# A ring of eight rows of mixing weights, and two projections in groups of 64 columns

## The chip, the core and the metric

The kernel runs on one core of one Trainium2 chip. The metric is the device time of one execution in microseconds. A profile shows each engine of the core: TensorE (PE, with its weight loads as PEld), VectorE (DVE), ScalarE (ACT), GpSimd (POOL) and SyncE (SP, which only starts transfers here). All arithmetic is float32; the query-key products alone read operands that VectorE has rounded and split into a high and a low part (`fp32r`).

## The reference

The input `x` has 4 images of 64 channels and 96 x 96 pixels. Two layers follow each other, each added to its input.

```python
# layer 0: attention without softmax, then a gate per channel
h = groupnorm(x)                       # 32 groups of 2 channels
q, k, v = wq @ h, wk @ h, wv @ h       # 8, 8 and 64 channels, N = 9216 pixels
att = sigmoid(q.T @ k)                 # [N, N] per image
out = v @ att.T + h
x = x + out * sigmoid(mlp(mean(out)) + mlp(max(out)))
# layer 1: a spectral convolution
u = rfft2(groupnorm(x))                # along w, then along h
top = einsum('bchw,cohw->bohw', u[:, :, :16, :16], R_pos)
bot = einsum('bchw,cohw->bohw', u[:, :, -16:, :16], R_neg)
x = x + irfft2(zeros with top and bot put in)
```

Layer 0 is nearly all of the work: for every image a 9216 x 9216 matrix is made, put through a sigmoid and multiplied by the values. In layer 1 only 32 x 16 frequencies of each channel are kept, so its transforms are small matrix products. At each kept frequency a 64 x 64 complex matrix of its own mixes the channels. These mixing weights (`spec`) come to 32 rows of 512 KB, one for each frequency along h.

## The kernel before, in words

The images go through in two pairs; two images of 64 channels fill the 128 partitions. A pair has 18 blocks of 512 queries, so there are 36 blocks, and each block goes over 72 chunks of 128 keys for both images: 144 tiles of 128 keys by 512 queries.

The loop (`for t in range(T)`) handles a burst of 6 or 7 tiles at a time. `energies` (L432) multiplies keys by queries into PSUM banks, ScalarE's `sigmoids` (L443) writes the attention tiles to SBUF in two instructions, and `attend` (L461) multiplies values by earlier tiles. Values of image b are 64 columns wide, so the matmuls of the two images go in turn to columns 0 to 63 and 64 to 127 of the array and accumulate in one bank. The lists `DENSE`, `HALF` and `SPARSE` give the burst sizes of a block: a burst of 7 uses all banks, and a burst of 6 leaves one bank over (`bank_a`). Everything else that TensorE does goes through that bank: `mid[t]` and `end[t]` hold the side steps of burst t, and `put` hands a chain of steps to the next free bursts of 6. `later` tells the framework's scheduler not to issue a step before the last marked vector instruction. Within that, the scheduler decides the order of instructions on each engine: it works with its own estimate of when operands are there, and lets other ready work of the same engine go first.

The side steps that matter here:

- In the two `DENSE` blocks, `keys` (L392) and `values_of` (L401) make keys and values of a pair, a block of 512 pixels at a time. `values_of` has four matmuls in which 128 pixels are the stationary operand (128 columns) and `wv` the moving one. `queries` (L412), `keys` and `attend` each put their output in two halves of 64 partitions.
- Layer 1 of the first pair (`Hidden`) runs in the free bursts while the second pair's attention goes on. Its order is: transposes (L266), transform along w (L276), group statistics, transform along h (L303), mixing (`mix`, L203), transform back along h (`back_h`, L322) and back along w (`back_w`, L343), and the sum with the input.
- `mix(q, half)` takes four rows of weights, 4q to 4q + 3, each in a group of 32 columns of the array, and has eight matmuls (two column frequencies by four rows). VectorE moves the result to the buffer `vms` (L579, the lambda given as `move`); after the second half, four stores (L219) send it to the DRAM tile `vd`. There are eight q, so sixteen steps.
- `weights` (L314) loads rows on the sync queue. Four buffers are held, so the rows of q + 1 are asked for after the second half of q.
- The first pair's `x` isn't needed any more by then. `workspace` puts into its place the transformed input `ut`, four rows of weights, one `vms` buffer, and later `z`, the input of the transform back along w. Another buffer, tag `ah`, 16 KB per partition, holds the input of the transform along h and afterwards `vt`, the mixed frequencies.
- `back_w(i)` has one matmul of 128 columns with 384 moving columns for every four image rows; 24 of them. VectorE (L345) adds the layer's input, and the sync queue stores it.

The second pair's layer 1 follows after the loop and has nothing to hide behind (from L640 on).

Of the kernel before, what the change touches and what calls it, by code (L numbers as in the profile page):

```python
# [33 lines left out]
F32 = mybir.dt.float32  # L34
# [6 lines left out]
P = 128  # L41
B, C, H, W = 4, 64, 96, 96
# [4 lines left out]
KW = 16  # L47
KH = 32
# [11 lines left out]
U = KH * KW * 4  # L60
UPAD = 4 * SIDE
# [20 lines left out]
def tile_kernel(ctx: ExitStack, tc: tile.TileContext, x, cst, late, spec, out):  # L82
    nc = tc.nc
# [10 lines left out]
    xs = []  # L94
# [11 lines left out]
    def named(name, rows=P):  # L106
        return cs[:rows, PLACE[name]]
# [128 lines left out]
    class Hidden(Layer1):  # L236
# [7 lines left out]
            self.ad = dram.tile([H, 2 * KW, P], F32, tag=f"ad{p}", name=f"ad_{p}")  # L244
            self.zd = dram.tile([H, 2 * KW, 2, C], F32, tag=f"zd{p}", name=f"zd_{p}")

        def place_of_vt(self):
            return self.work.tile([P, KW * C], F32, tag="ah", name=f"vt_{self.p}")

        def result(self, s):  # L250
            p, cols = self.p, bass.ts(s, STRIP)
# [82 lines left out]
        def back_w(self, i, x1d):  # L334

            s = i // 2
            cols = bass.ts(s, STRIP)
            if i % 2 == 0:
                self.old = self.work.tile([P, STRIP], F32, tag="old", bufs=2,
                                          name=f"x1_{self.p}_{s}")  # L340
                nc.sync.dma_start(self.old, x1d[:, cols])
            py = self.bank(f"py_{self.p}_{i}")
            nc.tensor.matmul(py[:, :4 * W], self.z[:, i, :], named("gw"), start=True, stop=True)  # L343
            o = self.old[:, bass.ts(i % 2, 4 * W)]
            nc.vector.tensor_tensor(o, py[:, :4 * W], o, ALU.add)  # L345
            if i % 2:
                nc.sync.dma_start(outf[bass.ts(self.p, P), cols], self.old)


    with tc.tile_pool(name="work", bufs=1) as work, \  # L350
# [9 lines left out]
        at = attp.tile([P, 14, NB], F32, tag="at", name="at")  # L360
# [3 lines left out]
        def bank_a(name):  # L364
            return banks[:, spare[0], :]
# [17 lines left out]
        def later(step):  # L383
            with tc.issue_after(mark[0].ins):
                step()
# [11 lines left out]

        def values_of(p, s):
            pp = bank_a(f"pv_{p}_{s}")
            for i in range(4):  # L400
                nc.tensor.matmul(pp[:, bass.ts(i, P)], xs[p][:, bass.ts(4 * s + i, P)],  # L401
                                 named("wv"), start=True, stop=True)
            nc.vector.tensor_tensor(  # L403
                vT[:, 4 * s:4 * s + 4, :], pp.rearrange("p (i m) -> p i m", m=P),
                named("bv").unsqueeze(1).to_broadcast([P, 4, P]), ALU.add)

        def queries(p, n):
            pq = bank_a(f"pq_{p}_{n}")
            half = NB // 2
            for e in range(2):  # L410
                rows = bass.ts(e, P // 2)
                nc.tensor.matmul(pq[rows, :half], named("wq")[:, rows],  # L412
                                 xs[p][:, n * NB + e * half:n * NB + (e + 1) * half],
                                 start=True, stop=True)
            qu, qh = halves(pq[:, :half], named("bq"), f"q_{p}_{n}")
            q = qp.tile([P, NB], F32R, tag="q", name=f"q_{p}_{n}")
            for e in range(2):
                rows, cols = bass.ts(e, P // 2), bass.ts(e, half)
                low_or_high(q[rows, cols], qu[rows, :], qh[rows, :], low_sb[rows, 0:1])
                for b in range(2):  # L420
                    to, of = 64 * (1 - e) + 32 * b, 64 * e + 32 * b
                    nc.vector.tensor_copy(q[to:to + 32, cols], q[of:of + 32, cols])  # L422
            return q
# [59 lines left out]
        def after(p):  # L483

            f = small.tile([P, 2], F32, tag="f", name=f"f_{p}")
            hid = small.tile([2 * R, 2], F32, tag="hid", name=f"hid_{p}")
            gate = small.tile([P, 1], F32, tag="gate", name=f"gate_{p}")

            def means():
                tot = small.tile([P, 1], F32, tag="tot", name=f"tot_{p}")  # L490
                nc.vector.tensor_reduce(tot, sums[p], AX.X, ALU.add)
                nc.vector.tensor_scalar(f[:, 0:1], tot, 1.0 / N, None, ALU.mult)
                nc.vector.tensor_reduce(f[:, 1:2], maxs[p], AX.X, ALU.max)

            def hidden():
                ph = bank_a(f"ph_{p}")
                nc.tensor.matmul(ph[:2 * R, 0:2], named("w1"), f, start=True, stop=True)
                nc.vector.tensor_scalar(hid, ph[:2 * R, 0:2], 0.0, None, ALU.max)

            def gates():  # L500
                pg = bank_a(f"pg_{p}")
                nc.tensor.matmul(pg[:, 0:2], named("w2", 2 * R), hid, start=True, stop=True)
                gsum = small.tile([P, 1], F32, tag="gsum", name=f"gsum_{p}")
                nc.vector.tensor_reduce(gsum, pg[:, 0:2], AX.X, ALU.add)
                nc.scalar.activation(gate, gsum, AF.Sigmoid)

            return gate, [means, hidden, gates], f
# [6 lines left out]
        keys(0, 0)  # L514
        q = queries(0, 0)
        values_of(0, 0)
        later(norm0[2])
        keys(0, 1)
        values_of(0, 1)

        pattern = [DENSE] + [SPARSE] * (NBLK - 2) + [DENSE] + [HALF] * 12
# [10 lines left out]
        end = [[] for _ in range(T)]  # L532
# [3 lines left out]
        def put(t, steps, every=1):  # L536

            for step in steps:
                t = next(f for f in free if f >= t)
                free.remove(t)  # L540
                mid[t] += [lambda step=step: later(step)]
                t += every
            return t

        ask = {}
        for n in range(1, NPAIR * NBLK):
            t = begins[n] - 4
            if pattern[n - 1] is DENSE:
                end[t] += [lambda n=n: ask.update({n: queries(n // NBLK, n % NBLK)})]
            else:  # L550
                t = [f for f in free if f < begins[n] - 1][-1]
                free.remove(t)
                mid[t] += [lambda n=n: ask.update({n: queries(n // NBLK, n % NBLK)})]
        for s in range(2, NBLK):
            end[s - 2] += [lambda s=s: keys(0, s)]
            mid[s - 1] += [lambda s=s: values_of(0, s)]
            if s + 1 < NBLK:
                end[s - 2] += [lambda s=s: later(norm0[s + 1])]
# [8 lines left out]
        for s in range(NBLK):  # L567
            tiles = TILES * (NBLK - 1) + 8 * (s + 1)
            t = next(t for t in range(T) if done[t] >= tiles)
# [9 lines left out]
        l1 = Hidden(0, gate, bank_a, lambda dst, src: nc.vector.tensor_copy(dst, src), work)  # L579
        x1d = dram.tile([P, N], F32, tag="x1", name="x1d")  # L580
        for s in range(NSTRIP):
# [3 lines left out]
        t = put(first + 9, [step for m in range(H // 16) for step in [  # L585
            lambda r=r: l1.transposes(r) for r in range(4 * m, 4 * m + 4)] + [
                lambda m=m: l1.along_w(m)]])
        t = put(t, l1.stats_steps(), 2)

        def workspace():  # L590
            ws = xpool.tile([P, N], F32, tag="x0", name="ws")
            l1.ut = ws[:, :U + UPAD]
            at = 2080
            l1.wts = [ws[:, at + 1024 * i:at + 1024 * (i + 1)] for i in range(4)] * (KH // 4)
            l1.vms = [ws[:, at + 4096:at + 5120]] * (KH // 4)
            l1.z = ws[:, at:at + 3072].rearrange("q (h m) -> q h m", m=P)
            l1.weights(range(4))

        end[t] += [workspace]
        t = put(t + 2, [lambda i=i: l1.along_h(i) for i in range(4)], 2)  # L600
        end[t] += [lambda: later(l1.constant_mode)]

        def mixing(q, half):
            l1.mix(q, half)
            if half and q + 1 < KH // 4:
                l1.weights(range(4 * q + 4, 4 * q + 8))

        t = put(t + 1, [lambda q=q, half=half: mixing(q, half)
                        for q in range(KH // 4) for half in range(2)])
        t = put(t + 5, [lambda i=i: l1.back_h(i // 4, i // 2 % 2, i % 2) for i in range(8)])  # L610
        t = put(t + 5, [lambda i=i: l1.back_w(i, x1d) for i in range(H // 4)])
# [13 lines left out]
        for s in range(NSTRIP):  # L625
            tiles = TILES * (NPAIR * NBLK - 1) + 2 * (STRIP // P) * (s + 1)
            t = next(t for t in range(T) if done[t] >= tiles)
# [5 lines left out]
        for t in range(T):  # L633
            n = block[t]
            spare[0] = n % 2 * 7
            if t + 1 < T:
                if starts[t + 1] == 0:
                    q = ask[n + 1]
# [12 lines left out]
        gate, steps, f = after(1)  # L651
# [4 lines left out]
    with tc.tile_pool(name="tail", bufs=1, reuse_waits="tile") as tail, \  # L656
# [6 lines left out]
        def place_of(tag, name):  # L663

            return tail.tile([P, KW * C], F32, tag=tag, name=name)
# [17 lines left out]
        def occupy(n, behind, pool):  # L683
# [3 lines left out]
            with tc.issue_after(behind.ins):  # L687
                for _ in range(n):
# [3 lines left out]
        l1 = Layer1(1, gate, lambda name: small_bank.tile([P, NB], F32, tag="m", name=name),  # L692
                    evacuate, (nc.sync, nc.gpsimd, nc.scalar))
# [12 lines left out]
        for s in range(NSTRIP):  # L706
# [7 lines left out]
            n, i = divmod(s, NSTRIP // NSQ)  # L714
# [6 lines left out]
            if i < NSTRIP // NSQ - 1:  # L721
# [7 lines left out]
                                 stop=(n == NSQ - 1 and part == 1))  # L729
# [13 lines left out]
        for i in range(9):  # L743
            h = NSLOT + 9 + i
# [14 lines left out]
        t = place_of("s", "t")  # L759
# [29 lines left out]
        for i in range(4):  # L789
            for e in range(2):  # L790
                for b in range(2):
                    rows = bass.ts(b, 2 * KH)
# [3 lines left out]
                        start=True, stop=True)  # L796
# [10 lines left out]
        for g in range(SQ // HG):  # L807
            py = py_bank.tile([P, NSQ, NB], F32, tag="y", name=f"py_{g}")
            for i in range(HG):
                for j in range(NSQ):  # L810
                    rows = bass.ts(j, SQ)
# [93 lines left out]
```

## Time and profile before

The median is 3162.33 us of 3 runs (3162.15 to 3162.39). The profiled execution spans 3160.8 us.

| what | us | share of the span |
|---|---|---|
| TensorE matmul | 3116.3 | 99% |
| TensorE weight loads | 1157.4 | 37% |
| ScalarE | 2424.2 | 77% |
| VectorE | 397.7 | 13% |
| GpSimd | 24.5 | 1% |
| values times attention, L461 | 2415.9 | 76% |
| energies, L432 | 577.6 | 18% |
| value projections, L401 | 43.8 | 1.4% |
| mixing of the first pair, L203 | 30.0 | 0.9% |
| back along w, L343 | 21.9 | 0.7% |

A row of the profile names line, engine, operation and tiles. One float32 matmul leaves two matmul records, one of the energies leaves one. In the timeline, records of the same line are merged into one row while no other comes between: the columns are the start, the time from the first start to the last end, and the number of records. As matmuls overlap, the length of such a row reaches into the next; what a group costs is the distance from its start to the start of the next group. The first pair's mixing runs from 1988 to 2191 us, its transform back along w from 2331 to 2562 us, and the two dense blocks are the first (from 29 us) and the nineteenth one (key and value projections of the second pair up to 1528 us).

### The profile page before, as it was taken

The numbers are of one execution on the slowest core, as the hardware profiler recorded it, in microseconds if no ns is written. First come the engines' busy times: TensorE is split into PE (matmuls) and PEld (weight loads), VectorE is DVE, ScalarE is ACT, GpSimd is POOL, SyncE is SP. The second block draws the span as 40 slices with busy tenths as digits, with TensorE's granted clock in tenths as the row PEclk, the third lists the DMA queues.
The fourth block names the chain that finished last, engine by engine and source line by source line (L and its number), as shares of the span: only waits on it lengthen the run. The fifth ranks groups of instructions, "written<-read, shape, count | busy, mean of one in ns | idle before, by whom it ended". The sixth has DMA issues, their size and how long they took to land.

```text
span 3160.8 us, 42345 instructions
## 1 busy us (share of the span) xinstructions
PE 3116.3 (99%) x18850; PEld 1157.4 (37%) x18850; DVE 397.7 (13%) x838; ACT 2424.2 (77%) x1585; POOL 24.5 (1%) x49
## 2 busy tenths in 40 slices
PE   6999999999999999999999999999999999999998
PEld 3433333333333333334333334333333333333336
DVE  5300000000000000003231111000101100000015
ACT  3788888888888888886777777756777778888871
POOL 0000000000000000000000000000000010000001
PEclk9999999999999999999999999999999999999998
DMA  3000000000000000000120010122211030000026
GB/s 141 1 1 1 1 1 1 1 1 1 1 1 1 1 1 1 1 1 1 40 94 8 7 41 1 61 94 67 31 30 41 31 128 1 1 1 1 6 64 222
DMA packets 39158, 88.82 MB, mean 28 GB/s; under 512 B 10336, under 2 KB 17248, under 8 KB 38880
## 3 DMA queue, kind: packets, MB, share of 16 engines
q1 hardware_dynamic: 31856, 61.88, 6.3%
q0 software_dynamic: 5344, 19.27, 1.6%
q10 hardware_dynamic: 1776, 4.97, 0.4%
q8 instruction: 147, 2.41, 0.3%
q14 instruction: 35, 0.29, 0.0%
HBM read 62.77 MB, written 23.33 MB: 27 GB/s over the span
## 4 chain that ended last, share of the span: by engine, by line
PE 97%; DVE 1%; DMA 1%; issue 0%; ACT 0%; SPq 0%; POOL 0%; ACTq 0%; DVEq 0%
PE banks L461 74%; PE banks L432 16%; PE banks L401 1%; PE banks L203 1%; PE banks L412 1%; PE banks L343 1%; PE banks L392 1%; DMA x<-in_x_dram 0%; PE py L812 0%; PE pv L203 0%; PE banks L266 0%; DVE x L162 0%; DMA old<-in_x_dram 0%; DVE xt L711 0%; PE banks L322 0%; PE banks L303 0%
## 5 line engine op out<-in xcount | busy, mean ns | idle before, releaser
L443 ACT ACTIVATE at<-banks 128x1536 f32<-128x1536 f32 (+1 forms) x1548 | 2404.0, 1597 | 656.3 <-PE banks L432 564.3
L461 PE MATMUL banks<-at,vT 128*64 128x512 f32 (+1 forms) x11728 | 2415.9, 550 | 0.0
L461 PEld LDWEIGHTS banks<-at,vT 128*64 128x64 f32 x11728 | 777.1, 136 | 1361.3 <-issue 1303.6
L432 PE MATMUL banks<-q,kT 32*128 32x512 f32 x5184 | 577.6, 454 | 2.3 <-ACT at L443 1.2
L432 PEld LDWEIGHTS banks<-q,kT 32*128 32x128 f32 x5184 | 235.1, 183 | 481.2 <-issue 304.1
L466 DVE SCALAR_TENSOR_TENSOR x<-banks,x 128x512 f32<-128x512 f32 x36 | 24.9, 692 | 898.1 <-PE banks L461 898.1
L372 DVE TENSOR_SCALAR full_q<-banks,cs 128x256 f32<-128x256 f32 x36 | 17.4, 484 | 854.0 <-PE banks L412 854.0
L401 PE MATMUL banks<-cs,x 128*128 128x128 f32 x288 | 43.8, 297 | 1.5 <-DVE full_q L372 0.6
L401 PEld LDWEIGHTS banks<-cs,x 128*128 128x128 f32 x288 | 36.6, 199 | 16.2 <-DVE full_k L372 14.6
L422 DVE CAST q<-q 32x256 fp32r<-32x256 f32 x144 | 40.9, 284 | 3.9
L345 DVE TENSOR_TENSOR x<-banks,x 128x384 f32<-128x384 f32 x24 | 13.4, 558 | 200.7 <-PE banks L343 160.6
L579 DVE COPY xT<-banks 96x512 f32<-96x512 f32 x24 | 16.5, 686 | 167.4 <-PE banks L266 167.4
L380 DVE SCALAR_TENSOR_TENSOR q<-high_q,cs,full_q 64x256 fp32r<-64x256 f32 x72 | 34.6, 480 | 2.4
L579 DVE COPY ws<-banks 128x512 f32<-128x512 f32 x16 | 11.1, 692 | 181.4 <-PE banks L203 171.9
L203 PE MATMUL banks<-ws 128*32 128x256 f32 x256 | 30.0, 387 | 0.0
L372 DVE TENSOR_SCALAR full_k<-banks,cs 128x256 f32<-128x256 f32 x36 | 17.4, 484 | 98.4 <-PE banks L392 98.4
L403 DVE TENSOR_TENSOR vT<-banks,cs 128x512 f32<-128x512 f32 x36 | 24.9, 692 | 9.4 <-PE banks L401 9.2
L392 PE MATMUL banks<-x,cs 128*64 128x256 f32 x144 | 23.9, 396 | 1.6 <-DVE x L149 1.5
L468 DVE TENSOR_REDUCE maxs<-x 128x1 f32<-128x512 f32 x36 | 24.7, 686 | 1.2
L412 PE MATMUL banks<-x,cs 128*64 128x256 f32 x144 | 23.9, 410 | 0.6 <-DVE full_k L372 0.6
L474 DVE BATCH_NORM_STATS2 stats<-x 128x6 f32<-128x512 f32 x36 | 22.2, 680 | 8.1 <-DMA x<-in_x_dram 8.1
L719 PE MATMUL pa<-xt,lc 128*128 128x256 f32 x72 | 18.8, 422 | 3.6 <-DVE xt L711 2.6
(115 smaller groups left out, 441.9 us busy)
## 6 DMA issues: line engine op xcount, KB each, us to landing
ws<-in_spec_dram SPq DMA_DIRECT2D x32, 512.0 KB
x<-in_x_dram SPq DMA_DIRECT2D x15, 512.0 KB
out_dram<-x SPq DMA_DIRECT2D x18, 384.0 KB
w<-in_spec_dram POOLq DMA_DIRECT2D x10, 512.0 KB, 6.5
old<-in_x_dram SPq DMA_DIRECT2D x12, 384.0 KB
x1d<-x SPq DMA_DIRECT2D x12, 384.0 KB
x<-x1d SPq DMA_DIRECT2D x12, 384.0 KB
w_early<-in_spec_dram POOLq DMA_DIRECT2D x9, 512.0 KB, 8.0
```

The costliest lines, as they stand in the source:

```text
L203: self.last = nc.tensor.matmul(pv[bass.ts(g, 32), :].rearrange("q (n k o) -> q n k o", n=SIDE, o=C)[:, :, k, :], self.ut[:, at:at + 32], s ...
L343: nc.tensor.matmul(py[:, :4 * W], self.z[:, i, :], named("gw"), start=True, stop=True)
L372: nc.vector.tensor_scalar(u, src, bias, None, ALU.add)
L380: mark[0] = nc.vector.scalar_tensor_tensor(dst, h.bitcast(F32), is_low, u, ALU.mult, ALU.add)
L392: nc.tensor.matmul(pp[cols, :NB // 2], named("wk")[:, cols], src[:, e, :, :], start=True, stop=True)
L401: nc.tensor.matmul(pp[:, bass.ts(i, P)], xs[p][:, bass.ts(4 * s + i, P)], named("wv"), start=True, stop=True)
L412: nc.tensor.matmul(pq[rows, :half], named("wq")[:, rows], xs[p][:, n * NB + e * half:n * NB + (e + 1) * half], start=True, stop=True)
L422: nc.vector.tensor_copy(q[to:to + 32, cols], q[of:of + 32, cols])
L432: nc.tensor.matmul(banks[:, bank_of(t) + i - starts[t], :], kT[r:r + 32, i // 4, :], q[r:r + 32, :], start=True, stop=True)
L443: nc.scalar.activation(at[:, of + lo:of + hi, :], banks[:, bank + lo:bank + hi, :], AF.Sigmoid)
L461: nc.tensor.matmul(acc[half, cols], vT[:, j, half], at[:, place(2 * pair + b), cols], start=(j == 0), stop=(j == NCH - 1))
L579: l1 = Hidden(0, gate, bank_a, lambda dst, src: nc.vector.tensor_copy(dst, src), work)
```

## The change

There are three edits, of two kinds.

The ring: the workspace now holds five rows of weights. When the transform along h has read its input, the buffer `ah` is taken again as a room for three more rows and for `vt`. This makes eight buffers, and the rows of q + 2 are asked for after the second half of q. So a row's load has a whole q more of time before it is used.

The halves: a value projection's 128 pixels, and the 128 rows (two images of 64 channels) of the transform back along w, are taken as two stationary operands of 64 columns, which go to the two halves of the array like `attend`'s. The number of products is the same; there are twice as many matmuls and weight loads, each half as wide.

```diff
-        def place_of_vt(self):
-            return self.work.tile([P, KW * C], F32, tag="ah", name=f"vt_{self.p}")
+        def more_room(self):
+            room = self.work.tile([P, 2 * KW * P], F32, tag="ah", name=f"room_{self.p}")
+            rooms = [room[:, bass.ts(i, KW * C)] for i in range(4)]
+            self.wts = (self.wts + rooms[:3]) * (KH // 8)
+            self.place_of_vt = lambda: rooms[3]
...
-            nc.tensor.matmul(py[:, :4 * W], self.z[:, i, :], named("gw"), start=True, stop=True)
+            for b in range(2):
+                nc.tensor.matmul(py[bass.ts(b, C), :4 * W], self.z[:, i, bass.ts(b, C)],
+                                 named("gw"), start=True, stop=True)
...
             for i in range(4):
-                nc.tensor.matmul(pp[:, bass.ts(i, P)], xs[p][:, bass.ts(4 * s + i, P)],
-                                 named("wv"), start=True, stop=True)
+                for e in range(2):
+                    nc.tensor.matmul(pp[bass.ts(e, P // 2), bass.ts(i, P)],
+                                     xs[p][:, bass.ts(2 * (4 * s + i) + e, P // 2)],
+                                     named("wv"), start=True, stop=True)
...
-            at = 2080
-            l1.wts = [ws[:, at + 1024 * i:at + 1024 * (i + 1)] for i in range(4)] * (KH // 4)
-            l1.vms = [ws[:, at + 4096:at + 5120]] * (KH // 4)
-            l1.z = ws[:, at:at + 3072].rearrange("q (h m) -> q h m", m=P)
-            l1.weights(range(4))
+            rows = [ws[:, U + UPAD + KW * C * i:U + UPAD + KW * C * (i + 1)] for i in range(6)]
+            l1.wts = rows[:5]
+            l1.vms = [rows[5]] * (KH // 4)
+            l1.z = ws[:, U + UPAD:U + UPAD + 3072].rearrange("q (h m) -> q h m", m=P)
+            l1.weights(range(5))
+
+        def more_room():
+            l1.more_room()
+            l1.weights(range(5, 8))
...
-        end[t] += [lambda: later(l1.constant_mode)]
+        end[t] += [more_room, lambda: later(l1.constant_mode)]
...
-            if half and q + 1 < KH // 4:
-                l1.weights(range(4 * q + 4, 4 * q + 8))
+            if half and q + 2 < KH // 4:
+                l1.weights(range(4 * q + 8, 4 * q + 12))
```

## The prediction

> **What bounds the kernel now.** I read the page's first part and the chain of the work that ended last, then PE's idle by releaser, then PE's timeline in the three stages that the change touches.
>
> ```profile
> PE 3116.3 (99%) x18850; PEld 1157.4 (37%) x18850; DVE 397.7 (13%) x838; ACT 2424.2 (77%) x1585; POOL 24.5 (1%) x49
> ...
> PE 97%; DVE 1%; DMA 1%; issue 0%; ACT 0%; SPq 0%; POOL 0%; ACTq 0%; DVEq 0%
> ```
>
> TensorE (PE) is 97% of the chain. All its waits together are 44.5 us (3160.8 - 3116.3), nearly all in the first 27 us and after 3072 us; inside the loop the only ones of note are 1.16 us at 1624 and 1.19 us at 2062. So a microsecond of PE's stream saved in the loop is a microsecond of the result, and what matters is the time from one group's start to the next, not the busy sums.
>
> The dense blocks (columns: start us, length us, engine, line). One burst with a key and a value projection:
>
> ```profile
> 1452.16 0.73 PE L432 MATMUL banks<-q,kT 32*128 32x512 f32 x6
> 1452.82 1.16 PE L401 MATMUL banks<-cs,x 128*128 128x128 f32 x8
> 1453.91 2.80 PE L461 MATMUL banks<-at,vT 128*64 128x512 f32 x12
> 1456.54 0.60 PE L392 MATMUL banks<-x,cs 128*64 128x256 f32 x4
> ```
>
> Each fp32 matmul leaves two records. L401's four full-width matmuls hold PE 1.09 us (1453.91 - 1452.82). L461's six value matmuls, in two groups of 64 columns in turn, take 2.63 us: 0.43 each.
>
> The mixing of the first pair. First the two steps of the first q, then a stretch of a later one:
>
> ```profile
> 1987.49 0.73 PE L432 MATMUL banks<-q,kT 32*128 32x512 f32 x6
> 1988.15 1.07 PE L203 MATMUL banks<-ws 128*32 128x256 f32 x16
> 1989.15 2.79 PE L461 MATMUL banks<-at,vT 128*64 128x512 f32 x12
> ...
> 1996.36 1.07 PE L203 MATMUL banks<-ws 128*32 128x256 f32 x16
> ```
>
> ```profile
> 2062.55 1.07 PE L203 MATMUL banks<-ws 128*32 128x256 f32 x16
> ...
> 2073.60 0.62 PE L203 MATMUL banks<-ws 128*32 128x256 f32 x2
> 2074.15 1.07 PE L461 MATMUL banks<-at,vT 128*64 128x512 f32 x2
> 2075.15 0.73 PE L432 MATMUL banks<-q,kT 32*128 32x512 f32 x6
> 2075.81 1.07 PE L461 MATMUL banks<-at,vT 128*64 128x512 f32 x2
> 2076.81 0.62 PE L203 MATMUL banks<-ws 128*32 128x256 f32 x2
> ...
> 2083.67 1.07 PE L203 MATMUL banks<-ws 128*32 128x256 f32 x16
> ```
>
> In one piece the eight L203 matmuls take 1.00 us. Scattered, a lone one takes 0.55 (2074.15 - 2073.60), and it tears a pair of value matmuls apart, so that a lone L461 takes 1.00 instead of 0.43. No wait stands here: the cost is in the order, which has the shape of weights arriving one row at a time.
>
> The transform back along w, 24 such:
>
> ```profile
> 2331.22 0.91 PE L343 MATMUL banks<-cs,ws 128*128 128x384 f32 x2
> 2332.06 2.80 PE L461 MATMUL banks<-at,vT 128*64 128x512 f32 x12
> ```
>
> That is 0.84 us for one 384-wide matmul.
>
> **What the Trainium skill says.** "TensorEngine Tiling (Array Packing)", Key Properties: different tiles run weight loads and matmuls in parallel, and changing the tiling mode drains the engine. The trace agrees: 64-column matmuls in turn come every 0.43 us where a lone one takes 1.00, and a last L461 matmul ahead of L432 takes 0.53 instead of 0.43, 0.10 for the drain. "TensorE: Matmul & The Clock Gate", Part 3, What overlaps: matmuls stay strictly in order. So an L203 that sits between two halves of an L461 pair really parts them, as seen.
>
> **Part 1, the ring.** Eight rows instead of four: five in the workspace and three in the room that held the input of the transform along h; rows for q+2 are asked for after q. The sizes and the work are the same. What moves is PE's order: in the changed program's instruction order all sixteen mixing groups stand as eight in a row, where before seven of the sixteen (the first half of every q but the first) were split into 1, 1, 1 and 5. The cost of a split: from the second half of one q to that of the next is 21.12 us (2083.67 - 2062.55), with 26 energy matmuls. One unsplit step, with 13 of them, is 8.21 us (1996.36 - 1988.15), so two are 16.42. Saved per q 4.70 us, times 7: 32.9, say 33.
>
> Will the weights be there? Four rows, 2.1 MB, land in about 10 us at the rate of this stage:
>
> ```profile
> 2040.00:2050.00 10.00, 10.00 (x68) 3.28 (x66) 2.08 (x4) 7.33 (x6) 0.00 (x0) 1.00 0.63 211
> ```
>
> (the last column is GB/s). Before, they were wanted 8.2 us after their request, which explains the split. Now they are wanted a whole q later, 24.6 us. Rows 5 to 7 go out when the transform along h ends (about 1974 before the shift) and are wanted at the second q, 30 us on, for 1.5 MB or some 8 us. One row of each batch (q+3's first) stands ahead of the intermediate's stores on the sync queue and waits for the second half of q+1, as those stores do through the vector copy; it adds about 2.5 us to their landing, against 8.2 us until the buffer is needed. So I cost the loads at nothing, hidden behind bursts. If all of them were late, the bound is the whole 33. ScalarE has room: two 1.45 us sigmoids per burst of 3.39 us (six energies and six values).
>
> **Part 2, value projections, 36.** Four 128-column matmuls become eight of 64 columns, in turn. L401 costs 1.09, and L461's first matmul after it shows 0.48 instead of 0.43: 0.05 to enter the 64-column mode. After: a 64-column matmul 512 wide costs 0.429 in turn, a 256-wide one 0.215 (L412, L392), a 64-wide one 0.058 (L303, where two weight loads sit behind so little streaming). For 128 wide that interpolates to 0.109. So 0.05 + 8 x 0.109 = 0.92, and nothing on the following L461, since its mode is already set; this is how L461 behaves after L412. Saved 1.09 + 0.05 - 0.92 = 0.22, or 0.17 if the entry is paid twice; 36 x 0.22 = 7.8 (6.1). The first two lie in a stage that VectorE's chain also holds, which could hide half a microsecond.
>
> **Part 3, back along w, 24.** Two of 64 columns: 0.05 + 2 x 0.322 = 0.69 against 0.84, and 0.05 on the next L461: 0.20 each, 24 x 0.20 = 4.8 (3.6 with the entry paid twice).
>
> Nothing else moves: the vector, scalar and queue work is the same in number, and the tail after 3072 us isn't touched. Sum: 33 + 7.8 + 4.8 = 45.6; 3162.3 - 45.6 = 3116.7, so 3117.
>
> **Rivals.**
> - The ring pays nothing: PE waits for weights where it was split before. For it: weights are requested in bursts on one queue. Against: 24.6 us of lead on 10 us. 3162.3 - 12.6 = 3150.
> - The halves pay nothing: twice as many weight loads bind at 128 columns of streaming. For it: a load's record is 136 ns (L412), longer than the 109 ns that a group then has for each of its passes. Against: L303 has loads of 138 ns, half the streaming, and still 58 ns a pass. 3162.3 - 33 = 3129.
> - The slower side: the halves run one after the other, each at the full-width price. Value projections add 4 x 0.223 = 0.89 x 36 = 32, back along w 24 x 0.64 = 15.4; 3162.3 - 33 + 47.4 = 3177. For it: lone 64-column matmuls do cost this. Against: L461, L392 and L412 all alternate and overlap.
>
> **How the numbers follow.** My forecast 0.86, ring alone failing 0.05, halves failing 0.06, slower 0.03. Within the forecast the parts can move by some 3 us downward in gain (entries paid twice, start hidden), or up by 5 if splits cost more where the sparse blocks begin. The range of 3110 to 3130 takes in the halves failing and leaves out the other two, 0.08, and a little of the edges. Faster 0.96, within 0.2% (6.3 us) 0.01, slower 0.03.
>
> **What would show it.** L203 as sixteen groups of 16 records with 8.2 us between the steps of a q and no wait for a transfer; value groups of 16 records in about 0.92 us; the back transform's 4 records in about 0.69; PE busy near 3071. I am wrong if PE shows waits for weights at L203, if an L401 successor's group stays near 1.09, or if the vector copy holds PE's bank once bursts are closer.

## The result, and the profile after

The changed kernel takes 3117.19 us (median of 4 runs, 3114.36 to 3118.38), against 3162.34 us before (3162.15 to 3162.39): a ratio of 0.9856, with a 95% interval of 0.9839 to 0.9873. The forecast was 3117.

The page after, its first part and the chain. Line numbers have moved: L401 is now L409, L432 is L441, L461 is L470, L343 is L348; L203 has kept its number.

```profile
PE 3072.2 (99%) x19186; PEld 1147.4 (37%) x19186; DVE 397.0 (13%) x838; ACT 2424.6 (78%) x1585; POOL 24.5 (1%) x49
...
PE 97%; DVE 1%; DMA 1%; issue 0%; POOL 0%; SPq 0%; ACT 0%; POOLq 0%; DVEq 0%
```

PE has 336 records more and 44.1 us less to do, and bounds the kernel as before. A dense burst and the start of the next one, after:

```profile
1448.13 1.09 PE L409 MATMUL banks<-cs,x 128*64 128x128 f32 x16
1449.05 2.75 PE L470 MATMUL banks<-at,vT 128*64 128x512 f32 x12
1451.63 0.60 PE L398 MATMUL banks<-x,cs 128*64 128x256 f32 x4
1452.16 0.73 PE L441 MATMUL banks<-q,kT 32*128 32x512 f32 x6
1452.82 1.09 PE L409 MATMUL banks<-cs,x 128*64 128x128 f32 x16
```

From start to start a group of value projections costs 0.92 us (was 1.09), and the six value matmuls behind it 2.58 (were 2.63): the step into the 64-column mode is paid once. The whole burst takes 4.69 us (1452.82 - 1448.13), 0.22 less than before.

The mixing, after: second half of one q, then the next q (the first row of a step whose rows lie in two buffers shows one record; the next rows hold the others).

```profile
2044.66 1.07 PE L203 MATMUL banks<-ws 128*32 128x256 f32 x16
2045.66 2.80 PE L470 MATMUL banks<-at,vT 128*64 128x256 f32 x16
...
2052.21 0.73 PE L441 MATMUL banks<-q,kT 32*128 32x512 f32 x6
2052.87 0.40 PE L203 MATMUL banks<-ws 128*32 128x256 f32 x1
...
2053.87 2.80 PE L470 MATMUL banks<-at,vT 128*64 128x512 f32 x12
...
2061.08 0.40 PE L203 MATMUL banks<-ws 128*32 128x256 f32 x1
```

One step takes 1.00 us (2053.87 - 2052.87), and second half to second half is 16.42 us, where it was 21.12. The back transform:

```profile
2290.49 0.87 PE L348 MATMUL banks<-cs,ws 128*64 128x384 f32 x4
2291.19 2.74 PE L470 MATMUL banks<-at,vT 128*64 128x512 f32 x12
```

0.70 us instead of 0.84. PE's waits, longest first, hold no wait for a row of weights at L203:

```profile
PE banks L132 <- DVE mv_l L128: 19.7, 1, 19.7
PE pz L806 <- DMA vt<-vd: 3.1, 1, 3.1
PE pa L732 <- DVE xt L724: 2.6, 2, 2.4
```

Where the time came from, by the start of each block's first energy matmul in the two traces (blocks counted from 0; the second dense block is block 17, so the eighteenth and not the nineteenth, and its last two value projections run on into block 18):

| stretch | what changed in it | us saved |
|---|---|---|
| start to block 19 | 36 value projections | 7.48 |
| block 19 to 23 | nothing; PE waits longer for VectorE | -0.44 |
| block 23 to 27 | mixing | 33.67 |
| block 27 to 30 | 24 back transforms | 4.66 |
| block 30 to the last energy matmul | nothing | -0.13 |
| behind it, the second pair's layer 1 | nothing | -1.07 |

That makes 44.2, the difference of the spans (3160.8 - 3116.6). The loss before block 23 is one wait, for VectorE's copy of the first pair's transposes (`xT`), first before the change, then after it:

```profile
1624.57 0.50 PE L432 MATMUL banks<-q,kT 32*128 32x512 f32 x1 [1.16 <-DVE xT L579]
1617.52 0.49 PE L441 MATMUL banks<-q,kT 32*128 32x512 f32 x1 [1.59 <-DVE xT L588]
```

The last row of the table was not followed up; it is less than the 4.0 us by which the runs of the changed kernel differ among themselves.

### The profile page after: what moved, and what is told of

The parts are those of the page before. It is cut to its first block, busy times and chain, and to the rows that moved or that the text cites. A ratio compares the mean times of both kernels' runs of the same rounds, so it can differ in the third digit from the quotient of the medians.

```text
span 3116.6 us, 43034 instructions
## 1 busy us (share of the span) xinstructions
PE 3072.2 (99%) x19186; PEld 1147.4 (37%) x19186; DVE 397.0 (13%) x838; ACT 2424.6 (78%) x1585; POOL 24.5 (1%) x49
## 3 DMA queue, kind: packets, MB, share of 16 engines
q10 hardware_dynamic: 1776, 4.97, 0.4%
## 4 chain that ended last, share of the span: by engine, by line
PE 97%; DVE 1%; DMA 1%; issue 0%; POOL 0%; SPq 0%; ACT 0%; POOLq 0%; DVEq 0%
PE banks L470 74%; PE banks L441 16%; PE banks L409 1%; PE banks L421 1%; PE banks L348 1%; PE banks L398 1%; PE banks L203 1%; DMA x<-in_x_dram 0%; PE py L825 0%; PE banks L270 0%; DVE x L162 0%; DMA old<-in_x_dram 0%; DMA vd<-vm 0%; DVE xt L724 0%; PE banks L326 0%
## 5 line engine op out<-in xcount | busy, mean ns | idle before, releaser
L470 PE MATMUL banks<-at,vT 128*64 128x512 f32 (+1 forms) x11728 | 2395.2, 549 | 0.0
L470 PEld LDWEIGHTS banks<-at,vT 128*64 128x64 f32 x11728 | 780.4, 136 | 1348.9 <-issue 1294.1
L441 PE MATMUL banks<-q,kT 32*128 32x512 f32 x5184 | 571.4, 454 | 1.6 <-DVE xT L588 1.6
L441 PEld LDWEIGHTS banks<-q,kT 32*128 32x128 f32 x5184 | 232.9, 182 | 472.3 <-issue 301.5
L409 PE MATMUL banks<-cs,x 128*64 128x128 f32 x576 | 41.6, 287 | 1.5 <-DVE full_k L378 0.6
L409 PEld LDWEIGHTS banks<-cs,x 128*64 128x64 f32 x576 | 32.3, 141 | 16.2 <-DVE full_k L378 14.6
L725 ACT ACTIVATE vT<-x,less 128x768 f32<-128x768 f32 x12 | 11.2, 934 | 12.4 <-DVE x L162 8.4
```

Of the source, the lines that this page charges most:

```text
L409: nc.tensor.matmul(pp[bass.ts(e, P // 2), bass.ts(i, P)], xs[p][:, bass.ts(2 * (4 * s + i) + e, P // 2)], named("wv"), start=True, stop=True)
L441: nc.tensor.matmul(banks[:, bank_of(t) + i - starts[t], :], kT[r:r + 32, i // 4, :], q[r:r + 32, :], start=True, stop=True)
L470: nc.tensor.matmul(acc[half, cols], vT[:, j, half], at[:, place(2 * pair + b), cols], start=(j == 0), stop=(j == NCH - 1))
```

## The experiments

My theory: PE's stream in the loop is the time. The ring saves by letting mixing steps stand whole in PE's order, the halves save by letting two column groups take turns, and the two are independent. Rivals: the parts lean on each other; the mixing had lost its time to the transfers themselves; the number of buffers or the line that asks for rows is what counts; narrow matmuls are cheaper in themselves.

| run | us, median | range of runs | ratio to the kernel before, run beside it, 95% |
|---|---|---|---|
| ring alone | 3132.78 | 3128.84 to 3133.58 | 0.9901, 0.9886 to 0.9916 |
| halves alone | 3150.20 | 3149.56 to 3150.92 | 0.9958, 0.9944 to 0.9973 |
| six rows | 3127.96 | 3126.96 to 3129.31 | 0.9889, 0.9872 to 0.9905 |
| four rows, steps apart | 3131.81 | 3130.81 to 3133.71 | 0.9901, 0.9886 to 0.9916 |
| four rows, steps kept whole | 3140.05 | 3139.81 to 3141.06 | 0.9927, 0.9910 to 0.9943 |
| request one q ahead | 3118.30 | 3116.45 to 3120.59 | 0.9857, 0.9843 to 0.9872 |
| half by half | 3132.58 | 3130.47 to 3132.72 | 0.9901, 0.9886 to 0.9915 |
| back along h, 64 + 32 | 3123.74 | 3121.44 to 3126.42 | 0.9877, 0.9861 to 0.9894 |
| back along h, 64 + 64 | 3118.36 | 3116.49 to 3119.95 | 0.9854, 0.9840 to 0.9869 |
| back along h, 3 x 32 | 3118.37 | 3117.32 to 3121.13 | 0.9857, 0.9840 to 0.9873 |

### Each part alone

The ring alone is the change with these lines taken out, and the full-width matmuls of before in their place:

```diff
-            for b in range(2):
-                nc.tensor.matmul(py[bass.ts(b, C), :4 * W], self.z[:, i, bass.ts(b, C)], ...
...
-                for e in range(2):
-                    nc.tensor.matmul(pp[bass.ts(e, P // 2), bass.ts(i, P)], ...
```

> The ring of eight rows alone; value projections and the transform back along w as before. My theory: sixteen mixing steps in one piece each, and nothing of the halves: 3162.3 - 33 = 3129 us (3127 to 3132). Rival (the parts are not additive: the ring gains only what the halves made room for, or the halves' shorter groups let the mixing run): clearly above 3135 us.

The halves alone are the kernel before with those two edits.

> The two edits in groups of 64 columns alone; four rows of weights as before. My theory: 3162.3 - 7.1 - 4.7 = 3150.5 us (3149 to 3153), with the seven split mixing steps still there. Rival (non-additive parts): below 3145 us or above 3156 us.

The halves came out as expected, 3150.2. The ring came out at 3132.8 where I had 3129. Yet from block 23 to block 27 it saves 33.67 us, to the hundredth what the whole change saves there. What its traced run (3133.58 us) lost lies where it has no edit: 1.92 us in the first bursts and 1.98 us around 1620 to 1640. Most of the second is TensorE's clock. The windows of the ring alone (time; busy us of PE, PEld, DVE, ACT, POOL; granted clock; DMA share; GB/s):

```profile
1610.00:1620.00 10.00, 10.00 (x57) 3.01 (x55) 7.39 (x13) 7.95 (x6) 0.00 (x0) 1.00 0.45 144
1620.00:1630.00 10.00, 8.54 (x51) 3.54 (x49) 2.88 (x5) 6.16 (x5) 0.00 (x0) 0.91 0.69 193
1630.00:1640.00 10.00, 10.00 (x55) 3.25 (x54) 0.69 (x1) 6.72 (x5) 0.00 (x0) 0.92 0.08 31
```

PE waits 1.46 us there for VectorE's `xT`, 0.30 more than the kernel before at the same place, and then the clock stands at half for 3.4 us: 0.09 and 0.08 of 10 us are lost, 1.7 us. The kernel before keeps 1.00. In the first bursts the matmuls take double the time for longer, as at half the clock: five records take 2.82 us in the ring alone,

```profile
37.41 2.82 PE L466 MATMUL banks<-at,vT 128*64 128x512 f32 x5
```

and 1.50 us in the kernel before:

```profile
37.22 1.50 PE L461 MATMUL banks<-at,vT 128*64 128x512 f32 x5
```

The clock column shows 1.00 there in both kernels, so that this loss is the clock's too isn't shown. Without the two losses the traced run would be near 3129.7, and the fastest of the four took 3128.84. The parts add up: 33.67 and, in the halves alone, 7.48 up to block 19 and 4.68 from 27 to 30.

### How much lead the rows need, and what gives it

Six rows:

```diff
-            self.wts = (self.wts + rooms[:3]) * (KH // 8)
+            self.wts = ((self.wts + rooms[:1]) * 6)[:KH]
...
-            if half and q + 2 < KH // 4:
-                l1.weights(range(4 * q + 8, 4 * q + 12))
+            if half:
+                l1.weights(range(4 * q + 6, min(4 * q + 10, KH)))
```

> The whole change but with six rows of weights instead of eight, so that two of a q's four rows are early and two late. In the program's order the seven steps that were split 1, 1, 1, 5 now stand as 3 and 5. My theory (the cost is lone matmuls and torn pairs in the order): one extra piece instead of three costs some 1.3 to 1.7 us a step, so 3117 + 9 to 12 = 3126 to 3129 us. Rival (the cost is the weights' own arrival, so that half of the rows late means about half of the loss): 3117 + 16 = 3133 us or more. Rival (any late row costs the whole): 3150 us.

Measured 3128.0, inside the first range. In the mixing stretch six rows save 22.66 us instead of 33.67: 11.0 us for seven steps in two pieces, 1.57 each. The trace shows such a step:

```profile
2056.25 0.63 PE L203 MATMUL banks<-ws 128*32 128x256 f32 x6
2056.82 2.79 PE L470 MATMUL banks<-at,vT 128*64 128x512 f32 x10
2059.53 1.05 PE L203 MATMUL banks<-ws 128*32 128x256 f32 x10
2060.51 1.07 PE L470 MATMUL banks<-at,vT 128*64 128x512 f32 x2
```

The two pieces hold PE for 0.57 and 0.98 us instead of 1.00 together, and the sixth value matmul, parted from its pair, costs 1.01.

Four rows with the steps apart, beside the halves (m < 4 pulls four q away from their predecessors):

```diff
-        t = put(t + 1, [lambda q=q, half=half: mixing(q, half)
-                        for q in range(KH // 4) for half in range(2)])
+        t += 1
+        for m in range(KH // 4):
+            for half in range(2):
+                t = put(t, [lambda m=m, half=half: mixing(m, half)],
+                        3 if half and m < 4 else 1)
```

> The halves with four rows of weights, and the mixing steps of the first four q pulled apart, so that each q after these four begins about 15 us after its rows were asked for instead of 8. In the program's order four of the seven splits are gone. My theory (lead time against the 10 us that four rows take is what counts, not the number of buffers): 3150.5 - 4 x 4.75 = 3131.5 us (3130 to 3134). Rival (eight buffers are what counts): 3150 us, as with the halves alone.

Measured 3131.8. No buffer was added, and four of the seven splits are gone with 19.87 us up to block 27, 4.97 each. Lead is what counts; buffers are one way to it. The steps of this run, two whole q, then a split one:

```profile
2050.10 1.07 PE L203 MATMUL banks<-ws 128*32 128x256 f32 x16
2058.31 1.07 PE L203 MATMUL banks<-ws 128*32 128x256 f32 x16
2073.73 1.07 PE L203 MATMUL banks<-ws 128*32 128x256 f32 x16
2081.95 1.07 PE L203 MATMUL banks<-ws 128*32 128x256 f32 x16
...
2141.89 1.07 PE L203 MATMUL banks<-ws 128*32 128x256 f32 x16
2150.11 0.62 PE L203 MATMUL banks<-ws 128*32 128x256 f32 x2
2152.95 0.62 PE L203 MATMUL banks<-ws 128*32 128x256 f32 x2
2155.59 0.62 PE L203 MATMUL banks<-ws 128*32 128x256 f32 x2
2157.99 1.05 PE L203 MATMUL banks<-ws 128*32 128x256 f32 x10
```

Between second half and first half lie 15.4 us (2073.73 - 2058.31) in the first case and 8.2 (2150.11 - 2141.89) in the other.

The request one q ahead, with all eight buffers:

```diff
-            l1.weights(range(5))
+            l1.weights(range(4))
...
-            l1.weights(range(5, 8))
...
-            if half and q + 2 < KH // 4:
-                l1.weights(range(4 * q + 8, 4 * q + 12))
+            if half and q + 1 < KH // 4:
+                l1.weights(range(4 * q + 4, 4 * q + 8))
```

> The whole change with eight rows of buffers, but the request for the rows put back to one q ahead in the source, and only rows 0 to 4 asked for at the workspace's start minus one (0 to 3). Theory: the loads are held by the buffers alone, since the scheduler sends a load as soon as its buffer is free; the order of the instructions is the change's, so 3117 us. Rival (the line that asks two q ahead is what brings the lead): the splits come back, 3150 us.

Measured 3118.3, with 33.67 us in the mixing stretch again. The place of the request in the source is of no account: in the two traces the instructions of all engines, and the sync queue's requests, stand in the same order. A load isn't held by `later`, so the scheduler can send it as soon as its buffer is free.

### Is it the order or the transfers?

In the kernel before, the rows that the last pieces of a split step were waiting for had landed earlier. Its windows in the first split step (last column GB/s):

```profile
2000.00:2010.00 10.00, 10.00 (x52) 3.17 (x50) 0.00 (x0) 6.14 (x5) 0.00 (x0) 1.00 0.55 191
2010.00:2020.00 10.00, 10.00 (x52) 3.56 (x53) 1.67 (x4) 5.40 (x4) 0.00 (x0) 1.00 0.01 2
```

and its timeline:

```profile
2010.05 0.62 PE L203 MATMUL banks<-ws 128*32 128x256 f32 x2
...
2012.88 1.05 PE L203 MATMUL banks<-ws 128*32 128x256 f32 x10
```

Nothing of weight moves after 2010 (in windows of 1 us, nothing after 2007), while two of the four pieces start then. The order, fixed in advance, was more cautious than the transfers. To price it, four rows again, with the halves, but the burst's value matmuls held behind the mixing step:

```diff
+            held, mixed[0] = mixed[0], None
-            attend(items[:old])
+            with tc.issue_after(held.ins) if held else nullcontext():
+                attend(items[:old])
             if t + 1 < T:
                 sigmoids(t + 1)
-            attend(items[old:])
+            with tc.issue_after(held.ins) if held else nullcontext():
+                attend(items[old:])
...
             l1.mix(q, half)
+            mixed[0] = None if half else l1.last
```

> The halves with four rows of weights, as in the run of the halves alone, but the value matmuls of a burst are held behind the mixing step in the order, so that the seven split steps stand as 1 and 7 and TensorE really waits for the rows. This tells the order's price from the price of the transfers. By the trace of the kernel before, the four rows had landed some 10 us after the second half of a q, and the next first half is due 8.2 us after it: a wait of about 2 us, 2 to 2.5 with the piece that stays split. My theory (most of the 4.75 us a q was the split order, not the transfer): 3117 + 7 x 2 to 2.5 = 3131 to 3135 us, with PE's waits on the transfers standing in the trace. Rival (the split order cost no more than the transfers would have): 3150 us as before. Rival (the rows are there in time, the scheduler only feared they were not): 3119 us.

Measured 3140.05: between my range and the first rival's. (This run, as traced, also lost some 3.6 us in the first bursts and to the clock at 1621, as the ring alone did; the mixing stretch is free of that.) There it saves 15.04 of the 33.67, so a q still costs 18.6 / 7 = 2.66 us too much instead of 4.81. PE's waits name ScalarE (ACT) first and the rows only for 2.0 us:

```profile
PE banks L436 <- ACT at L447: 5.8, 7, 0.8
...
PE banks L203 <- DMA ws<-in_spec_dram: 2.0, 5, 1.2
```

But one step, with a row of its weight loads (PEld) below, shows that the rows come last:

```profile
2061.21 0.62 PE L203 MATMUL banks<-ws 128*32 128x256 f32 x2
2062.66 0.50 PE L436 MATMUL banks<-q,kT 32*128 32x512 f32 x3 [0.83 <-ACT at L447]
2063.08 1.68 PE L203 MATMUL banks<-ws 128*32 128x256 f32 x14
2064.69 2.80 PE L465 MATMUL banks<-at,vT 128*64 128x512 f32 x12
...
2063.71 0.57 PEld L203 LDWEIGHTS banks<-ws 128*32 128x32 f32 x10 [0.48 <-DMA ws<-in_spec_dram]
```

The first matmul still stands alone, and three energy matmuls are put behind it that wait 0.83 us for ScalarE. After that wait the weight loads of the last five matmuls still wait 0.48 us for a row. It is so in all seven steps: in each the weight loads wait for a row before the last five matmuls, 0.30 to 1.72 us, and PE's own five waits lie inside these.

A step in one piece, waiting for the same row, would have ended no sooner, so the wait for ScalarE hides part of the wait for rows. From start to end the seven steps take 2.3 to 3.7 us more than the 1.00 us of a step whose rows are there (2064.69 - 2061.21 - 1.00 = 2.48 in this one), 19.3 us together, which covers the 18.6. So the 33.67 us have two parts of like size: 15.04 us are the price of the split order alone, since they go while the rows are asked for as late as before, and up to 18.6 us are what late rows cost a TensorE that waits for them. The ring takes away both. That most of the cost was the order's, as I expected, isn't borne out: it is 2.15 of 4.81 us a q.

### Why halves are cheaper

The order of the eight value projections, otherwise unchanged:

```diff
-            for i in range(4):
-                for e in range(2):
+            for e in range(2):
+                for i in range(4):
```

> The whole change, but the eight matmuls of a value projection in another order: first the four into partitions 0 to 63, then the four into 64 to 127. Products, loads and widths are the same. My theory (halves pay only because two column groups take turns): matmuls of one half follow each other at the full-width price of about 0.22 us, so a group takes some 1.7 us instead of 0.92; 36 x 0.75 = 27, so 3117 + 27 = 3144 us. Rival (narrow matmuls are cheaper in themselves, or the weight load of a half hides either way): 3117 us.

Measured 3132.6: the same matmuls in another order cost 15.4 us more, which is more than the halves of the value projections had saved. Narrow matmuls aren't cheaper in themselves. My figure of 27 was too high, though. The timeline of this run, from one value group to the next:

```profile
1494.40 1.25 PE L409 MATMUL banks<-cs,x 128*64 128x128 f32 x13
1495.38 0.64 PE L470 MATMUL banks<-at,vT 128*64 128x512 f32 x1
1495.49 0.49 PE L409 MATMUL banks<-cs,x 128*64 128x128 f32 x3
...
1499.57 1.25 PE L409 MATMUL banks<-cs,x 128*64 128x128 f32 x13
```

A burst takes 5.17 us, 0.48 more than after the change; I had 0.75. The rows show one reason: the first value matmul (1495.38) starts while three records of L409 are still to come (1495.49), so the last projection overlaps with it. A like overlap at the turn from one half to the other is likely; the rows don't tell the halves apart. Then six of eight are paid singly, by estimate 6 x 0.218 + 0.05 = 1.36 against 0.92, 0.44 more.

### One more place for halves

The transform back along h has eight matmuls of 96 columns, 1.03 us each. In two groups:

```diff
-            nc.tensor.matmul(pz[:H, :], named("gh")[rows, bass.ts(e, H)],
-                             self.vt[rows, bass.ts(half, KW // 2 * C)], start=True, stop=True)
+            for lo, hi in ((0, C), (C, H)):
+                nc.tensor.matmul(pz[lo:hi, :], named("gh")[rows, e * H + lo:e * H + hi],
+                                 self.vt[rows, bass.ts(half, KW // 2 * C)],
+                                 start=True, stop=True)
```

> The whole change, and the eight matmuls of the transform back along h (96 columns, 512 moving) also in two column groups, of 64 and 32 columns. Theory, from the entry and drain seen at the other two: 1.03 us a step becomes 0.05 + 2 x 0.43 = 0.91, and the value matmul behind it saves its 0.05: 8 x 0.17 = 1.4 us, 3116 us, which only the profile can tell. Rival (32 columns of 64 run as a third group and pair badly): 3117 us or above, the step near 1.03 us.

Measured 3123.7: slower, as the rival had it, though the step isn't near 1.03 us. It takes 1.97 us:

```profile
2202.18 2.04 PE L327 MATMUL banks<-room,cs 64*64 64x512 f32 x4
2204.15 2.79 PE L472 MATMUL banks<-at,vT 128*64 128x512 f32 x12
```

The two don't overlap at all. The profile names the row by its first matmul; the second has 32 columns. To tell the unequal widths from the 64 contracted rows, both groups with 64 columns, and then three groups of 32:

```diff
+            gh = PLACE["gh"].start + e * H
+            for lo in (0, C):
+                nc.tensor.matmul(pz[lo:lo + C, :], cs[rows, gh + lo:gh + lo + C], ...
```

> As the run with the transform back along h in groups of 64 and 32 columns, but both groups of 64: the second one has 32 columns of other constants beside its own 32, whose output rows nobody reads. If equal widths are what lets two groups take turns, a step takes 0.05 + 2 x 0.43 = 0.91 us instead of 1.97 (64 and 32) or 1.03 (96): 3117 - 1.4 = 3116 us, seen in the profile. Rival (a contraction of 64 rows is what keeps them apart, or the row position): about 1.97 us a step again, 3123 us.

```diff
+            for lo in (0, 32, 64):
+                nc.tensor.matmul(pz[lo:lo + 32, :],
+                                 named("gh")[rows, e * H + lo:e * H + lo + 32], ...
```

> The same transform in three groups of 32 columns. If equal widths are enough: the three overlap, a step takes about 0.9 us (the transform along w, four groups of 32 columns and 512 moving, takes 0.9 to 1.0), 3116 us. Rival (the row position or the 64 rows keep them apart): three times 0.97, about 2.9 us a step, 3117 + 15 = 3132 us.

With two of 64:

```profile
2207.40 1.07 PE L328 MATMUL banks<-room,cs 64*64 64x512 f32 x4
2208.40 2.80 PE L473 MATMUL banks<-at,vT 128*64 128x512 f32 x12
```

With three of 32:

```profile
2203.41 1.06 PE L327 MATMUL banks<-room,cs 64*32 64x512 f32 x6
2204.40 2.79 PE L472 MATMUL banks<-at,vT 128*64 128x512 f32 x12
```

1.00 to 1.01 and 0.99 us: they overlap, so it was the unequal widths that kept the groups apart, and not the 64 rows or the row position. That fits the Trainium skill, "TensorEngine Tiling (Array Packing)", Key Properties: a change of tiling mode drains the engine. It would also explain why 0.91 wasn't reached: with 64 rows the step is in another mode than the value matmuls, and the drain would stay; no run here separates this. The gain of 0.02 to 0.04 us a step is nothing against 3117; both runs are level with the change, and no version here beats it.

## Why the prediction was right

- The ring, 33 us: measured 33.67. The cost of a split (4.70 forecast, 4.81 measured) and the number of splits, seven, both held. The loads are hidden, as I had them: no wait for a row stands in the trace after.
- The reason that I gave for the lead was half right. Lead does decide (steps apart). But I put it down to the line that asks for q + 2, and the run with that line put back shows that the free buffers alone set it.
- "The weights were wanted 8.2 us after their request" as the cause of the split: in the kernel before the price stood in the order, without a wait, as I read it. But the order is not the whole of what the ring repairs. With the steps kept whole only 15.04 of the 33.67 us came back, and the rest is covered by rows that are late.
- "About 10 us at the rate of this stage": in the seven steps kept whole the last rows could be used 10.4 to 12.0 us after the start of the second half, so the figure held, but the rate was only part of it. In the kernel before, the sync queue sends three of the four rows behind the stores of the result (at 1998.36), 3.75 us after that start (2000.11 - 1996.36). No run here puts them ahead of the stores.
- The value projections, 7.8 us: 7.48, of which the first block has 3.64. A group in the second dense block saves 0.22 where the rows above show it, as forecast, and 0.21 on average (3.84 / 18). A longer wait for VectorE near 1618 us, which I had at nothing, gives back 0.44.
- The back transform, 4.8 us: 4.66, or 0.19 a step against 0.20. The step into 64-column mode is paid once, as chosen; the other end of that choice (3.6 and 6.1) didn't come.
- The rival that the halves pay nothing because their weight loads bind: refuted by the groups of 0.92 us. The rival that they run one after the other: refuted for the change, and seen where widths differ.
- What I didn't foresee: losses to the clock, or what looks like it. Ring alone, steps kept whole and back along h with 64 + 64, as traced, lost about 4 us each away from their edits, in the first bursts and at half the clock after the wait for `xT`. The runs of the changed kernel spread over 4.0 us, and those of the kernel before over 5.2 in the later comparisons (3161.49 to 3166.73), so the spread isn't the change's own; that it is the clock's too isn't shown.
- The sum, 3116.7, lies nearer to the median of 3117.19 than the runs of the changed kernel lie to each other (4.0 us). That closeness is luck; the parts are what was forecast.

## What to carry to other kernels

When PE bounds a loop and shows no waits, look for split groups in its timeline: a lone matmul of a column group costs as much as a full-width one (0.22 us each at 128 moving columns, half by half and before the change), and it parts the pairs around it. What tears them can be a late operand in the scheduler's estimate. Give such loads lead, by more buffers or by spacing the steps, rather than only forcing the order, which brought back less than half here. When several waits share a step, look at the weight loads too: the wait that comes last sets its end. Matmuls for column groups pay when they take turns, all of one width and next to work of the same mode.

## What the runs showed of the hardware

- Two column groups of unequal width (64 and 32, 512 moving) don't overlap: a step of both takes 1.97 us, against 1.00 to 1.01 for two of 64 and 0.99 for three of 32.
- Waits for `xT` in PE's stream of 1.46 (ring alone), 1.63 (steps kept whole) and 1.73 us (64 + 64) were followed by half the clock for 3.4 us, which costs 1.7 us. Those of 1.16 (before), 1.59 (after), 1.78 (64 + 32) and 2.02 us (halves alone) at the same place were not, so the length doesn't decide. The Trainium skill, "TensorE: Matmul & The Clock Gate", Part 1, has a free-running activity window of 3413 ns and puts the fall to half after a whole idle window. The length of 3.4 us agrees; the fall does not, since these waits are about half a window or less. What decides stays open.
- A 64-column matmul of 128 moving columns came every 0.109 us in turn ((0.92 - 0.05) / 8), with weight loads recorded at 0.141 us each.
